# Reuse waits per tile instead of per pool in a four-layer network on one core

## The chip, the core and the metric

The kernel runs on one core of one Trainium2 chip. The metric is the device time of one execution in microseconds (us), the median of several runs. An execution under the hardware profiler gives the trace from which all views of the profile are taken. Engines are named as the profile names them: PE is TensorE (PEld its weight loads), DVE is VectorE, ACT is ScalarE, POOL is GpSimd, and SP issues most of the DMAs. DMAs can also be issued from ACT's and POOL's queues.

## What is computed

The input x has 8 blocks of 512 tokens with 128 features, all float32. Four layers follow, each "macaron" style: half of a feed-forward network is added, then attention, then the same feed-forward network once more by half. In outline:

```python
for layer in range(4):
    x = x + 0.5 * ffn[layer](layernorm(x))
    x = x + attn[layer](layernorm(x))
    x = x + 0.5 * ffn[layer](layernorm(x))
```

The parts differ by layer:

- Layer 0: attention with 16 heads of 8 and a learned bias by relative position (clipped at 128 either way), whole 512 x 512 softmax. Its feed-forward part has 8 experts of 176, top 2, and a shared expert of 352.
- Layer 1: causal attention with 16 heads, value width 64. Its feed-forward part holds a small attention over 8 columns, a layer normalisation and 8 experts of which one is applied to each token.
- Layer 2: an associative scan over the tokens (two 128 x 128 products and an RMS normalisation per combination) in place of softmax attention. Its feed-forward part sends each token to one of 8 experts of 512 with a squared ReLU.
- Layer 3: full attention with 16 heads. Its feed-forward part has 64 experts of 96, top 8 with a capacity of 64 tokens for each expert, and a shared expert. Tokens beyond an expert's capacity are dropped.

## The kernel before

The residual X stays in SBUF as one tile of 128 partitions x 32 token tiles x 128 features for the whole run. A block is four token tiles. All stages run on all 8 blocks, one stage after another, as run() (L2069) lists them. Start times in the trace: ffn0 (0, with attention0's preparations between its steps), attention0 (378), ffn0 (1179), ffn1 (1517), attention1 (1861), ffn1 (2520), ffn2 (2862), attn2 (3089), ffn2 (3257), ffn3 (3437), attention3 (3622), ffn3 (4230), end (4418).

**Pools.** Each stage opens pools of SBUF tiles and a pool of PSUM banks and closes them at its end. The next stage's pools are laid over the memory that the last one left. Within a pool a tag names a ring of buffers (`bufs`), handed out in program order. A few pools live throughout: `const` (X, identity, weight slot a), `small` (statistics of the normalisations `ln_mv`, `ln_st`, `ln_rs`, two buffers each, L145 and L158 to L169) and `dram` (tables in DRAM). `late` holds weight slot b from the second ffn0 on.

**What waits.** A framework, Tile, puts the semaphores. When a pool covers memory of closed pools, the pool's tiles wait by default until the whole of those pools is released, that is, until the last instruction that used any tile of them has ended. Data that passes through X, and tiles of a living pool, have waits of their own in either case.

**What orders the instructions.** The kernel's code gives a program order. Tile schedules from it with a list scheduler, which may put an instruction of one engine ahead of an earlier one where nothing that it waits for stands against it, with the earlier lines going first. In the trace, L824 of attention3 (a copy of a bias out of slot b) runs at 2852.33, in ffn1. Each engine works its own list in order.

The lines that the prediction's steps touch:

- `stats` and `scale` (L158 to L175): a block's mean, variance, and the normalised tile `xn` of the next stage. `transpose4` (L180 to L188) turns it through a PSUM bank `mid` into `XT`.
- `ffn0` (L263): xn, gate, experts L323 to L335. PSUM pool `psum` from `banks` (L130): mid 2 banks, big 2 x 2, acc 2.
- `attention0` (L356, pools at L589): scores L501 in `ps_s`, transposes L525 and products L542 in banks of their own.
- `ffn1` (L1008): `half`, `spread_v`, then xn at L1040 (on ACT), transposes L1047, products L1073. Blocks are taken in two halves of four columns.
- `attention1` (L600): `mask` at L619 is the first tile, then statistics and xn; its output projections are L771.
- `ffn2` (L1349): statistics in a pool of its own (`s2`), a sort of the tokens by expert through DRAM (L1504), expert weights `wt` fetched on SP's queue (L1500), sorted tokens (L1525), copies `xst` (L1546), up L1553, ReLU L1559, down L1573, results added to X (L1612).
- `attn2` (L1627): pools `a2` (the sequences `seq0` and on) and `a2b` (xn and temporaries).
- `ffn3` (L1709): pools `f3` (`zero`, `keys` and other single tiles) and `f3b` (normalised tokens `xw`, weights of the experts, gathered tokens). `zero` is filled on POOL (L1723), and `clear` (L1742) writes it from ACT's queue over the DRAM table `parts`, two transfers of 1 MB for each of the first three blocks. The routing (L1771 to L1777) follows, then the experts, and at the end `collect` in the pool `f3c` (L2006 to L2021), which adds eight rows to each token. A second part of the routing and of the collection stands under a condition (`tc.If`) that is not taken here.
- `attention3` (L804): its own xn, a V tile filled by memset, and PSUM pool `ps3` with seven banks `one` and one `acc`.

Where tiles lie over each other, in kilobytes of a partition (worked out from the tile sizes, in the order of the pools): `ahead` 82.1 to 159.4, with PB's three buffers at 88.4 to 127.4. ffn0's XT 108.7 to 124.7 and f0's xn from 124.7. ffn1's `half`, xn and xt 108.7 to 122.7, hm 209.7 to 215.7. attention1's mask 108.7 to 110.7. ffn2's xn 124.7 to 140.8, s2 212.8 on (first time). attn2's seq0 124.7 to 140.8, a2b 156.7 to 170.8. ffn3's zero 124.7 to 132.7, f3b 154.7 to 220.7, f3c 124.7 to 152.7. attention3's V 124.7 to 140.7.

Of the kernel before, what the change touches and what calls it, by code (L numbers as in the profile page):

```python
# [65 lines left out]
class Slot:  # L66


    def __init__(self, flat):
        self.flat = flat  # L70
        self.off = 0
# [10 lines left out]
class Net:  # L82
    def __init__(self, ctx, tc, ins, out):
        self.tc, self.nc, self.ins, self.out = tc, tc.nc, ins, out
        nc = self.nc
        self.const = ctx.enter_context(tc.tile_pool(name="const", bufs=1))
        self.small = ctx.enter_context(tc.tile_pool(name="small", bufs=2))
        self.dram = ctx.enter_context(
            tc.tile_pool(name="dram", bufs=4, space=bass.MemoryType.DRAM)
        )  # L90
# [38 lines left out]
    @contextmanager  # L129
    def banks(self):  # L130

        with self.tc.tile_pool(name="psum", bufs=2, space=bass.MemoryType.PSUM) as p:
            self.psum = p
            yield
        self.psum = None

    @contextmanager
    def turned(self):

        with self.tc.tile_pool(name="turned", bufs=1) as p:  # L140
            self.XT = p.tile([P, NB, BT], F32, name="XT")
            yield
        self.XT = None
# [119 lines left out]
    def ffn0(self, ahead=()):  # L263

        nc, w = self.nc, self.w
        with self.tc.tile_pool(name="f0", bufs=2) as pool:
            wts = {}

            def prep(b):
# [86 lines left out]
    def attention0(self, pool, zero):  # L356
# [5 lines left out]
        with ExitStack() as ctx:  # L362
            psum = late = None
# [222 lines left out]
                at(4 * m + 6, lambda m=m: gather(m))  # L586
                at(4 * m + 8, lambda m=m: output(m))
            yield [f for n in range(-29, 0) for f in extra.get(n, [])]
            late = ctx.enter_context(self.tc.tile_pool(name="at0", bufs=2))  # L589
            psum = ctx.enter_context(self.tc.tile_pool(name="ps0", bufs=2, space=bass.MemoryType.PSUM))  # L590
            for n in range(N + 9):
                if n < N:
                    scores(n)
# [6 lines left out]
    def attention1(self):  # L600
# [2 lines left out]

        nc, w = self.nc, self.w
        with ExitStack() as ctx:
            pool = ctx.enter_context(self.tc.tile_pool(name="at1", bufs=2))
            psum = ctx.enter_context(self.tc.tile_pool(name="ps1", bufs=2, space=bass.MemoryType.PSUM))
            LAG, LAGV = 12, 3
            NU = NB * 4
            N = 8 * NU  # L610
# [193 lines left out]
    def attention3(self):  # L804
# [3 lines left out]

        nc, w = self.nc, self.w
        with ExitStack() as ctx:  # L810
            pool = ctx.enter_context(self.tc.tile_pool(name="at3", bufs=2))
            psum = ctx.enter_context(self.tc.tile_pool(name="ps3", bufs=1, space=bass.MemoryType.PSUM))
            self.psum = psum
            LAG, LAGV = 12, 3
            NU = NB * 4
# [192 lines left out]
    def ffn1(self):  # L1008
        nc, w = self.nc, self.w
        scale = 1.0 / math.sqrt(HD)  # L1010
        with ExitStack() as ctx:
            pool = ctx.enter_context(self.tc.tile_pool(name="f1", bufs=2))
            psum = ctx.enter_context(self.tc.tile_pool(name="ps1", bufs=2, space=bass.MemoryType.PSUM))

            def mid():
                return psum.tile([P, BT], F32, name="ps_mid", tag="mid", bufs=3)
# [332 lines left out]
    def ffn2(self, with_polar):  # L1349
# [3 lines left out]
        nc, w = self.nc, self.w  # L1353
        NE, KT, HC = 8, 39, 4
        with ExitStack() as ctx:
            pool = ctx.enter_context(self.tc.tile_pool(name="f2", bufs=2))
            small, self.small = self.small, ctx.enter_context(self.tc.tile_pool(name="s2", bufs=2))
            self.psum = ctx.enter_context(self.tc.tile_pool(name="ps2", bufs=2, space=bass.MemoryType.PSUM))
            extra = self.polar_steps(pool) if with_polar else []
            xs_table = self.table2  # L1360

# [264 lines left out]

    def attn2(self):  # L1627
        nc, w = self.nc, self.w
        with self.tc.tile_pool(name="a2", bufs=1) as pool, self.tc.tile_pool(name="a2b", bufs=2) as pool2:
            eps = pool.tile([P, 1], F32, name="eps")  # L1630
            nc.gpsimd.memset(eps, EPS_RMS)
            lens = [BT + 1]
# [76 lines left out]
    def ffn3(self, last):  # L1709
# [6 lines left out]
        ROWS = K3 * NTOK  # L1716
        HALF = NTOK // 2
        SOON = 3
        with self.tc.tile_pool(name="f3", bufs=1) as pool, self.tc.tile_pool(name="f3b", bufs=2) as pool2:
            table = self.table  # L1720
            parts = self.dram.tile([ROWS + NTOK, D], F32, name="parts", tag="parts", bufs=1)
            zero = pool.tile([P, 16 * D], F32, name="zero")
# [283 lines left out]
            fetch(1)  # L2006
            interleave([lambda n=n: group(n) for n in range(8)], [lambda i=i: shared(i) for i in range(NB + 3)])

        with self.tc.tile_pool(name="f3c", bufs=2) as pool:
            def collect(t):  # L2010
                c = pool.tile([P, K3, D], F32, name="co", tag="co", bufs=6)
                nc.sync.dma_start(
                    out=c.rearrange("p j d -> p (j d)"),
                    in_=parts[t * P * K3 : (t + 1) * P * K3, :].rearrange("(p j) d -> p (j d)", j=K3),
                )
                r = pool.tile([P, 4, D], F32, name="cr", tag="cr")
                nc.gpsimd.tensor_tensor(out=r, in0=c[:, 0:4, :], in1=c[:, 4:8, :], op=ALU.add)  # L2017
                nc.vector.tensor_tensor(r[:, 0:2, :], r[:, 0:2, :], r[:, 2:4, :], ALU.add)  # L2018
                nc.vector.tensor_tensor(r[:, 0, :], r[:, 0, :], r[:, 1, :], ALU.add)  # L2019
                x = self.X[:, t, :]  # L2020
                nc.vector.scalar_tensor_tensor(x, r[:, 0, :], 0.5, x, ALU.mult, ALU.add)  # L2021
                if last and t % 4 == 3:
                    self.store(t // 4)

            for t in range(4 * SOON):
                collect(t)
            with self.tc.If(more):
                for t in range(4 * SOON, NT):
                    collect(t)
# [38 lines left out]

    def run(self):  # L2069
        self.load("a", self.L0)  # L2070
        with self.tc.tile_pool(name="ahead", bufs=2) as ahead:
            with self.tc.tile_pool(name="blank", bufs=1) as pool:
                zero = self.ready2(pool)
                rest = self.attention0(ahead, zero.rearrange("p (k c) -> p k c", k=8))
                steps = next(rest)
                with self.turned(), self.banks():
                    self.ffn0(steps)
            for _ in rest:
                pass
        with self.tc.tile_pool(name="late", bufs=1) as late:  # L2080
            self.slots["b"] = late.tile([P, 6816], F32, name="slot_b")
            self.load("b", self.L1)
            with self.turned(), self.banks():
                self.ffn0()
            self.load("a", self.L2)
            self.ffn1()
            self.attention1()
            self.ffn1()
            self.load("b", self.L3)
            with self.turned():  # L2090
                self.ffn2(True)
                with self.banks():
# [148 lines left out]
```

## Time and profile before

| | |
|---|---|
| median of 3 runs | 4406.22 us (4403.34 to 4411.11) |
| profiled execution | 4419.59 us |
| its span in the trace | 4417.8 us |
| mean granted PE clock | 0.903 |
| ACT busy | 2086.6 us (47%) |
| POOL busy | 980.7 us (22%) |
| DMA | 331.79 MB, mean 75 GB/s |
| DMA `wt` (ffn2's expert weights) | 78 of 512 KB, 4.2 us to land |
| DMA `parts` from `zero` | 12 of 1024 KB, 11.7 us to land |

The page of the profile gives busy time for each engine, then the span in 40 slices of 110.4 us: a digit is the busy share in tenths (9 means 90% or more). PEclk in that table is the clock that TensorE was granted, in tenths of full speed. A line of the timeline has the start in us, the busy time, engine, line, operation, output and inputs, shape and count, and in brackets how long the engine had idled before it and what ended that. "DVEq" and "ACTq" are the queues of these engines, with register loads and DMA issues. A wait for several things is put down to the one that came last. In a row of the windows view, the stretch and its length are followed by busy time of PE, PEld, DVE, ACT and POOL with the count of instructions, the granted clock, DMA's busy share and GB/s.

### The profile page before, as it was taken

How to read it: one execution, taken by the hardware profiler on the slowest of the kernel's cores; microseconds unless marked ns; L12 is line 12 of the kernel's file. 1: busy time of each engine (PE TensorE's matmuls, PEld its weight loads, DVE VectorE, ACT ScalarE, POOL GpSimd, SP SyncE). 2: the span in 40 equal slices, each digit the busy share in tenths (PEclk: the TensorE clock that was granted, in tenths of full speed). 3: DMA queues.
4: the chain of work that ended last, by engine and by line, in shares of the span. 5: the costliest groups of instructions: out<-in, count | busy, mean ns of one | idle time of the engine just before them, and what ended most of it. 6: DMA issues, size and time to landing. Idle time of an engine off the chain costs nothing. (4 is left out here: it accounts for less than half of the span.)

```text
span 4417.8 us, 64316 instructions
## 1 busy us (share of the span) xinstructions
PE 3785.8 (86%) x23046; PEld 2065.0 (47%) x23046; DVE 2765.6 (63%) x7495; ACT 2086.6 (47%) x4422; POOL 980.7 (22%) x1270
## 2 busy tenths in 40 slices
PE   8999999999999868899999967868667359999946
PEld 3445666666544345434344444467347233333324
DVE  5655777777756566656656466656553556777654
ACT  2335877878533324377877623312213015555521
POOL 1001111111000265211111266143024350000026
PEclk9999999999999979989999979969668579999967
DMA  6006777777300000000000000035007430000035
GB/s 256 0 5 203 220 226 221 223 221 225 93 1 1 5 0 1 1 1 1 1 1 1 1 0 2 8 100 172 0 13 239 153 125 1 1 1 1 1 109 169
DMA packets 217613, 331.79 MB, mean 75 GB/s; under 512 B 19954, under 2 KB 188380, under 8 KB 213700
## 3 DMA queue, kind: packets, MB, share of 16 engines
q1 hardware_dynamic: 197284, 290.59, 20.5%
q0 software_dynamic: 9664, 19.84, 1.5%
q10 hardware_dynamic: 10336, 17.17, 1.0%
q8 instruction: 183, 3.00, 0.3%
q14 instruction: 146, 1.20, 0.1%
HBM read 182.71 MB, written 144.82 MB: 74 GB/s over the span
## 5 line engine op out<-in xcount | busy, mean ns | idle before, releaser
L509 DVE CUSTOM_DVE_ANT_0 ps_s<-ps_s,PB 128x512 f32<-128x512 f32 x512 | 352.3, 704 | 155.5 <-PE ps_s L501 73.8
L901 DVE TENSOR_REDUCE nm<-ps_one 128x1 f32<-128x512 f32 x512 | 328.9, 685 | 155.4 <-PE ps_one L895 140.3
L513 ACT ACTIVATE pn<-ps_s,nm 128x512 f32<-128x512 f32 x512 | 356.8, 697 | 104.8 <-DVE nm L509 104.8
L907 ACT ACTIVATE pt<-ps_one 128x512 f32<-128x512 f32 x512 | 277.6, 595 | 203.7 <-PE ps_one L895 157.8
L168 POOL TENSOR_TENSOR ln_rs<-ln_rs,mhalf 128x4 f32<-128x4 f32 x128 | 132.7, 1037 | 897.5 <-DVE ln_rs L167 887.4
L895 PE MATMUL ps_one<-KT,QT 32*128 32x512 f32 x1024 | 307.5, 662 | 0.8 <-ACT KT L857 0.8
L675 ACT ACTIVATE sc<-sc,nm 128x512 f32<-128x512 f32 (+3 forms) x512 | 285.8, 562 | 39.5 <-DVE nm L732 33.3
L525 PE MATMUL ps_one<-ident,pn 128*128 128x128 f32 x2048 | 293.3, 282 | 12.2 <-DVE y L562 9.8
L732 DVE CUSTOM_DVE_ANT_0 sc<-ps_one,mask 128x512 f32<-128x512 f32 (+3 forms) x512 | 232.3, 487 | 105.5 <-PE ps_one L723 86.3
L887 PE MATMUL ps_one<-Q,KT 32*128 32x512 f32 x1024 | 289.7, 639 | 0.0
L326 ACT ACTIVATE sg<-ps_big 128x512 f32<-128x512 f32 x224 | 132.3, 597 | 320.2 <-PE ps_big L324 300.0
L450 PE MATMUL ps_one<-rdiff,QT 32*128 32x256 f32 x940 | 267.4, 404 | 14.5 <-ACT pt L528 14.4
L525 PEld LDWEIGHTS ps_one<-ident,pn 128*128 128x128 f32 x2048 | 219.1, 141 | 122.2 <-ACT pn L513 37.4
L327 DVE TENSOR_TENSOR sg<-sg,ps_big 128x512 f32<-128x512 f32 x224 | 152.3, 684 | 194.1 <-ACT sg L326 192.4
L739 ACT ACTIVATE pt<-ps_one 128x512 f32<-128x512 f32 (+3 forms) x512 | 209.6, 431 | 101.0 <-PE ps_one L723 92.9
L323 PE MATMUL ps_big<-XT,slot_a 128*128 128x512 f32 x448 | 236.7, 610 | 12.2 <-DVE sg L327 12.2
L501 PE MATMUL ps_s<-KT,QT 32*128 32x512 f32 (+2 forms) x1024 | 237.3, 540 | 0.8 <-ACT E L454 0.7
L324 PE MATMUL ps_big<-XT,slot_a 128*128 128x512 f32 x448 | 233.2, 602 | 0.0
L723 PE MATMUL ps_one<-KT,QT 32*128 32x512 f32 (+3 forms) x1024 | 229.7, 494 | 3.5 <-ACT pt L739 2.8
L715 PE MATMUL ps_one<-Q,KT 32*128 32x512 f32 (+3 forms) x1024 | 226.2, 483 | 6.8 <-ACT KT L662 5.8
L335 PE MATMUL ps_acc<-h,slot_a 128*128 128x512 f32 x448 | 229.8, 596 | 0.4 <-DVE h L329 0.4
L456 POOL COPY E<-E 128x127 f32<-128x127 f32 (+1 forms) x256 | 88.6, 346 | 637.2 <-ACT E L454 631.5
(436 smaller groups left out, 8386.1 us busy)
## 6 DMA issues: line engine op xcount, KB each, us to landing
rel_rows<-E SPq DMA_DIRECT2D x192, 383.0 KB, 3.7
PB<-rel_rows SPq DMA_DIRECT2D x128, 384.0 KB, 3.4
wt<-in_f_w_dram SPq DMA_DIRECT2D x78, 512.0 KB, 4.2
PB<-rel_rows SPq DMA_DIRECT2D x128, 256.0 KB
table<-blank SPq DMA_DIRECT2D x16, 1032.0 KB, 17.8
rel_rows<-E SPq DMA_DIRECT2D x64, 256.0 KB, 3.2
parts<-zero ACTq DMA_DIRECT2D x12, 1024.0 KB, 11.7
co<-parts SPq DMA_DIRECT2D x24, 512.0 KB, 7.1
```

The source lines that it names most:

```text
L323: nc.tensor.matmul(out=gu[:, 0, :], lhsT=w["f0_g"][:, cs], rhs=self.XT[:, b, :], start=True, stop=True)
L324: nc.tensor.matmul(out=gu[:, 1, :], lhsT=w["f0_u"][:, cs], rhs=self.XT[:, b, :], start=True, stop=True)
L450: nc.tensor.matmul(out=ps[:, c * 256 : c * 256 + 256], lhsT=Q[u][rr, i * P : (i + 1) * P], rhs=rdiff[rr, :], start=True, stop=True, tile_p ...
L501: nc.tensor.matmul(out=s[:, k, far:BT], lhsT=qt[rr, i * P : (i + 1) * P], rhs=kt[rr, far:BT], start=True, stop=True, tile_position=(32 * g ...
L509: nc.vector.tensor_tensor_reduce(out=s[:, k, :], in0=s[:, k, :], in1=pb[:, k, PB_AT[i] : PB_AT[i] + BT], scale=-1.0, scalar=1e30, op0=ALU. ...
L513: nc.scalar.activation(pn[:, k, :], s[:, k, :], AF.Exp, bias=nm[:, k : k + 1], scale=-1.0)
L525: nc.tensor.transpose(ps[:, j * P : (j + 1) * P], pn[:, k, j * P : (j + 1) * P], self.ident)
L675: nc.scalar.activation(sc[:, k, 0:wd], sc[:, k, 0:wd], AF.Exp, bias=maxs[u % 2][:, i, g, HD : HD + 1], scale=-1.0, accum_out=SUMS[u][:, i, ...
L887: nc.tensor.matmul(out=tw[k], lhsT=K[uw][rr, j * P : (j + 1) * P], rhs=Q2[uw][rr, :], start=True, stop=True, tile_position=(32 * g, 0),)
L895: nc.tensor.matmul(out=ts[k], lhsT=Q[u][rr, i * P : (i + 1) * P], rhs=K[u][rr, :], start=True, stop=True, tile_position=(32 * g, 0),)
L901: nc.vector.tensor_reduce(maxs[u % 2][:, i, 2 * hp + k : 2 * hp + k + 1, HD], ts[k], AX.X, ALU.max, negate=True)
L907: nc.scalar.activation(PT[m][:, k, :], tw[k], AF.Exp)
```

## The change

Nearly every pool is opened with `reuse_waits="tile"`. With it, a tile that is laid over memory of a closed pool waits for the accesses to those old tiles whose bytes or banks it covers, and not for the whole pool. No computation, size, address or program order is edited. Of the pools, two keep the default: `a2b` (L1629) and `f3b` (L1719). The diff, cut to one place of each kind:

```diff
-        self.const = ctx.enter_context(tc.tile_pool(name="const", bufs=1))
-        self.small = ctx.enter_context(tc.tile_pool(name="small", bufs=2))
+        self.const = ctx.enter_context(tc.tile_pool(reuse_waits="tile", name="const", bufs=1))
+        self.small = ctx.enter_context(tc.tile_pool(reuse_waits="tile", name="small", bufs=2))
...
-        with self.tc.tile_pool(name="psum", bufs=2, space=bass.MemoryType.PSUM) as p:
+        with self.tc.tile_pool(reuse_waits="tile", name="psum", bufs=2, space=bass.MemoryType.PSUM) as p:
...
-            pool = ctx.enter_context(self.tc.tile_pool(name="f1", bufs=2))
-            psum = ctx.enter_context(self.tc.tile_pool(name="ps1", bufs=2, space=bass.MemoryType.PSUM))
+            pool = ctx.enter_context(self.tc.tile_pool(reuse_waits="tile", name="f1", bufs=2))
+            psum = ctx.enter_context(self.tc.tile_pool(reuse_waits="tile", name="ps1", bufs=2, space=bass.MemoryType.PSUM))
...
-        with self.tc.tile_pool(name="a2", bufs=1) as pool, self.tc.tile_pool(name="a2b", bufs=2) as pool2:
+        with self.tc.tile_pool(reuse_waits="tile", name="a2", bufs=1) as pool, self.tc.tile_pool(name="a2b", bufs=2) as pool2:
...
-        with self.tc.tile_pool(name="f3", bufs=1) as pool, self.tc.tile_pool(name="f3b", bufs=2) as pool2:
+        with self.tc.tile_pool(reuse_waits="tile", name="f3", bufs=1) as pool, self.tc.tile_pool(name="f3b", bufs=2) as pool2:
...
-        with self.tc.tile_pool(name="f3c", bufs=2) as pool:
+        with self.tc.tile_pool(reuse_waits="tile", name="f3c", bufs=2) as pool:
```

The same edit stands at `dram`, `turned`, `f0`, `at0`, `ps0`, `at1`, `ps1` (twice), `at3`, `ps3`, `f2`, `s2`, `ps2`, `ahead`, `blank` and `late`.

More of the change, by code (lines that the diff above doesn't have):

```diff
@@ L85, in __init__ @@
         nc = self.nc
-        self.const = ctx.enter_context(tc.tile_pool(name="const", bufs=1))
-        self.small = ctx.enter_context(tc.tile_pool(name="small", bufs=2))
+        self.const = ctx.enter_context(tc.tile_pool(reuse_waits="tile", name="const", bufs=1))
+        self.small = ctx.enter_context(tc.tile_pool(reuse_waits="tile", name="small", bufs=2))
         self.dram = ctx.enter_context(
-            tc.tile_pool(name="dram", bufs=4, space=bass.MemoryType.DRAM)
+            tc.tile_pool(reuse_waits="tile", name="dram", bufs=4, space=bass.MemoryType.DRAM)
         )
@@ L138, in turned @@
     def turned(self):
-        with self.tc.tile_pool(name="turned", bufs=1) as p:
+        with self.tc.tile_pool(reuse_waits="tile", name="turned", bufs=1) as p:
             self.XT = p.tile([P, NB, BT], F32, name="XT")
@@ L265, in ffn0 @@
         nc, w = self.nc, self.w
-        with self.tc.tile_pool(name="f0", bufs=2) as pool:
+        with self.tc.tile_pool(reuse_waits="tile", name="f0", bufs=2) as pool:
             wts = {}
@@ L588, in attention0 @@
             yield [f for n in range(-29, 0) for f in extra.get(n, [])]
-            late = ctx.enter_context(self.tc.tile_pool(name="at0", bufs=2))
-            psum = ctx.enter_context(self.tc.tile_pool(name="ps0", bufs=2, space=bass.MemoryType.PSUM))
+            late = ctx.enter_context(self.tc.tile_pool(reuse_waits="tile", name="at0", bufs=2))
+            psum = ctx.enter_context(self.tc.tile_pool(reuse_waits="tile", name="ps0", bufs=2, space=bass.MemoryType.PSUM))
             for n in range(N + 9):
@@ L605, in attention1 @@
         with ExitStack() as ctx:
-            pool = ctx.enter_context(self.tc.tile_pool(name="at1", bufs=2))
-            psum = ctx.enter_context(self.tc.tile_pool(name="ps1", bufs=2, space=bass.MemoryType.PSUM))
+            pool = ctx.enter_context(self.tc.tile_pool(reuse_waits="tile", name="at1", bufs=2))
+            psum = ctx.enter_context(self.tc.tile_pool(reuse_waits="tile", name="ps1", bufs=2, space=bass.MemoryType.PSUM))
             LAG, LAGV = 12, 3
@@ L810, in attention3 @@
         with ExitStack() as ctx:
-            pool = ctx.enter_context(self.tc.tile_pool(name="at3", bufs=2))
-            psum = ctx.enter_context(self.tc.tile_pool(name="ps3", bufs=1, space=bass.MemoryType.PSUM))
+            pool = ctx.enter_context(self.tc.tile_pool(reuse_waits="tile", name="at3", bufs=2))
+            psum = ctx.enter_context(self.tc.tile_pool(reuse_waits="tile", name="ps3", bufs=1, space=bass.MemoryType.PSUM))
             self.psum = psum
@@ L1011, in ffn1 @@
         with ExitStack() as ctx:
-            pool = ctx.enter_context(self.tc.tile_pool(name="f1", bufs=2))
-            psum = ctx.enter_context(self.tc.tile_pool(name="ps1", bufs=2, space=bass.MemoryType.PSUM))
+            pool = ctx.enter_context(self.tc.tile_pool(reuse_waits="tile", name="f1", bufs=2))
+            psum = ctx.enter_context(self.tc.tile_pool(reuse_waits="tile", name="ps1", bufs=2, space=bass.MemoryType.PSUM))
             def mid():
@@ L1355, in ffn2 @@
         with ExitStack() as ctx:
-            pool = ctx.enter_context(self.tc.tile_pool(name="f2", bufs=2))
-            small, self.small = self.small, ctx.enter_context(self.tc.tile_pool(name="s2", bufs=2))
-            self.psum = ctx.enter_context(self.tc.tile_pool(name="ps2", bufs=2, space=bass.MemoryType.PSUM))
+            pool = ctx.enter_context(self.tc.tile_pool(reuse_waits="tile", name="f2", bufs=2))
+            small, self.small = self.small, ctx.enter_context(self.tc.tile_pool(reuse_waits="tile", name="s2", bufs=2))
+            self.psum = ctx.enter_context(self.tc.tile_pool(reuse_waits="tile", name="ps2", bufs=2, space=bass.MemoryType.PSUM))
             extra = self.polar_steps(pool) if with_polar else []
@@ L2070, in run @@
         self.load("a", self.L0)
-        with self.tc.tile_pool(name="ahead", bufs=2) as ahead:
-            with self.tc.tile_pool(name="blank", bufs=1) as pool:
+        with self.tc.tile_pool(reuse_waits="tile", name="ahead", bufs=2) as ahead:
+            with self.tc.tile_pool(reuse_waits="tile", name="blank", bufs=1) as pool:
                 zero = self.ready2(pool)
@@ L2079, in run @@
                 pass
-        with self.tc.tile_pool(name="late", bufs=1) as late:
+        with self.tc.tile_pool(reuse_waits="tile", name="late", bufs=1) as late:
             self.slots["b"] = late.tile([P, 6816], F32, name="slot_b")
```

## The prediction

> **What bounds the kernel.** I read the engine totals first, then the 40 slices.
>
> ```profile
> span 4417.8 us, 64316 instructions
> ...
> PE 3785.8 (86%) x23046; PEld 2065.0 (47%) x23046; DVE 2765.6 (63%) x7495; ACT 2086.6 (47%) x4422; POOL 980.7 (22%) x1270
> ...
> PE   8999999999999868899999967868667359999946
> ...
> PEclk9999999999999979989999979969668579999967
> ```
>
> The reader should see two things. TensorE (PE) is busy 86% of the span, and where it reads 9 no pool wait can cost anything: the stage is bound by matmuls. The rest of the span, 632 us of idle PE, lies in the handovers from stage to stage, at slice 15, in slices 24 to 33 and in the last two; there the clock row falls too. The change can only act where a first tile of a new stage waits for the last user of old memory, so I then read the timeline at each handover of run().
>
> Releasers in these lines say what came last, not what was needed:
>
> ```profile
> 1178.55 0.86 DVE L175 TENSOR_SCALAR xn<-X,ln_mv,ln_rs 128x128 f32<-128x128 f32 x3 [2.01 <-PE ps_av L542]
> 1516.74 1.65 ACT L1040 ACTIVATE xn<-X,ln_nmr,ln_rs 128x128 f32<-128x128 f32 x4 [0.89 <-PE ps_mid L211]
> 1861.83 0.52 POOL L619 MEMSET mask<- 128x512 f32 x1 [1.77 <-DVE ln_mv L165]
> 2520.30 3.18 ACT L1040 ACTIVATE xn<-X,ln_nmr,ln_rs 128x128 f32<-128x128 f32 x8 [9.46 <-PE ps_one L771]
> 3622.38 3.57 DVE L175 TENSOR_SCALAR xn<-X,ln_mv,ln_rs 128x128 f32<-128x128 f32 x4 [0.61 <-DVEq L2027]
> 4230.72 1.80 POOL L1723 MEMSET zero<- 128x2048 f32 x1 [46.55 <-PE ps_one L955]
> ```
>
> In each, a memset or a normalisation that reads only X and its statistics starts as the old stage's last product or transpose ends. Neither reads that product; the memory is all they share. That is the wait to be split.
>
> **The change, handover by handover.** Nothing is computed that was not computed before; what may move is when first tiles are written. That work does move up when it may: in the trace L824 (attention3's `a_qb`) runs at 2852.33, in the middle of ffn1. What holds it afterwards is the last of three: the tile it covers, its PSUM bank, its data. The `small` tags (two buffers) are handed out in program order as well.
>
> 1. ffn0 to attention0 (378): the scores wait for the last E (L454), whose mid banks 0 and 1 are also the scores' first banks. 1.5 us; ends 0 and 2.
> 2. attention0 to ffn0 (1179): xn lies over PB buffers last read near 1167, and the mid banks are free by 1173.5. PE idles 0.46+0.69+0.72 = 1.9 us around its first transposes, and then runs four pairs L323/L324 at 1.73 to 2.06 us against 1.02, which is 3.6 more. 5.5 us; ends 0 and 7.
> 3. ffn0 to ffn1 (1517): f1's xn lies over XT, last read at 1511.9, so half 0 (its four tiles are final) can go. Tile 28 of X is final only at 1517.3. 4 us; ends 0 and 5.4 (1517.3 less 1511.9).
> 4. ffn1 to attention1 (1861): the mask covers `half`, read until 1861.2, and the statistics' small tags are taken until then. 1 us; ends 0 and 2.
> 5. attention1 to ffn1 (2520): ACT idled 9.46 us before xn. X of those tiles is long final, but the three mid banks were used by the last projections, free at 2515.2, 2518.1 and 2520.5, and PE works to 2520.2. xn, its copies and the next transposes move up by 4.5 us; ends 0 and 9.5.
> 6. ffn1 to ffn2 (2862): PE idles 8.21 us before 2868.66. DVE waits there for X of the last blocks, but the first four blocks are final by 2850, and the s2 statistics lie over hm buffers read until about 2858. DVE's start at 2865.05 moves under the tail. 4.5 us; ends 0 and 8.2.
> 7. ffn2 to attn2 (3089): `a2b` (L1629) is not given the option; its xn waits as before. 0.5 us; ends 0 and 1.
> 8. attn2 to ffn2 (3257): xn covers seq0, read until 3255.3. 1.5 us; ends 0 and 2.
> 9. ffn2 to ffn3 (3437): `f3b` keeps the old wait, so xw (L175 at 3437.87) stays. What moves is `zero`, in `f3`, and with it six clears of `parts` on ACT's queue.
>
> ```profile
> 3437.71 1.80 POOL L1723 MEMSET zero<- 128x2048 f32 x1 [0.73 <-DVE X L1612]
> 3441.93 10.72 ACTq L1742 DMA_DIRECT2D parts<-zero  x6
> 3453.15 0.42 DVE L1777 TENSOR_REDUCE r_s<-p 128x4 f32<-128x256 f32 x1 [7.43 <-ACT p L1771]
> ```
>
> These hold ACT for 10.72 us and through its exp leave DVE idle 7.43: that goes, 7.4 us gained. But `zero` covers ffn2's normalised tokens, last read by the sort at 3328, so the six may go at about 3332, beside the first experts. Two windows of ten microseconds show what they meet (PE, PEld, DVE, ACT, POOL busy, then clock, DMA share, GB/s):
>
> ```profile
> 3330.00:3340.00 10.00, 4.27 (x14) 2.77 (x14) 0.59 (x4) 1.18 (x2) 0.00 (x0) 0.50 0.63 178
> 3390.00:3400.00 10.00, 9.84 (x89) 9.65 (x88) 3.84 (x8) 4.66 (x8) 3.90 (x5) 1.00 0.98 326
> ```
>
> Six clears write 6.29 MB: 14.8 us of all DMA engines at the 426 GB/s of their own window, 19.3 at 326. From 3340 on the share is 0.92 to 1.00 and PE takes weights as they come (2.44 us waited for wt at 3337). Behind the clears in ACT's order stand the copies of sorted tokens (3334.79) and the relus (from 3339.28), for which PE waits. DMA is idle 3.7 of the 10 us to 3340, so I take 11 us lost (14.8 less 3.7). Net -3.5 us; ends +7.4 (they land after 3410, where the share is 0.32) and -18 (10.72 of ACT and 14.8 of DMA in turn, less 7.4).
>
> [...]
>
> 10. ffn3 to attention3 (3622): xn, transposes and the memsets of V may pass the last collect, but DVE is busy 8.3 of 10 us there and 9.0 in the next ten. Of ten microseconds I count 4; ends 0 and 10.
> 11. attention3 to ffn3 (4230): the clears lie over V of an early block and can go out while DMA is idle; the 3.51 us for which DVE waited at 4243.24 and part of the 1.80 memset go. xw keeps its wait. 4.5 us; ends 0 and 5.3.
>
> The sum is 1.5+5.5+4+1+4.5+4.5+0.5+1.5-3.5+4+4.5 = 28 us. The profiled execution took 4419.59 us (span 4417.8, 1.8 around it) and would take 4391.6: 0.63% less. On the median of 4406.22 this makes **4378**. All items at their good ends make 60 us; all at their bad ones, -18.
>
> **The clock at the handovers.** Two windows after the one at 1861 (same columns, five microseconds each):
>
> ```profile
> 1875.00:1880.00 5.00, 5.00 (x8) 1.00 (x6) 3.13 (x15) 4.00 (x16) 0.00 (x0) 0.50 0.00 0
> 1895.00:1900.00 5.00, 5.00 (x12) 1.66 (x15) 2.24 (x10) 1.97 (x8) 0.00 (x0) 0.50 0.00 0
> ```
>
> PE is busy throughout and the granted clock is still 0.50; it rises near 1903. So a shorter gap does not by itself bring the clock back, and I count none of it in the sum, except the four pairs of item 2. [...]
>
> **Rivals.**
> *A, little moves.* The small tags' order, the banks of the last products and the true data on X hold the first tiles about as long as the pool did. For it: items 1, 4, 7 and 8, where this is what I read. Against: 2, 3, 5, 11. Then some 5 us come back: 4401. That the option moves no instruction at all ends here too, at 4406.
> *B, slower.* The clears' landing place decides. If all six leave between 3332 and 3343 ahead of the copies in ACT's order, both prices are paid: -18 us. If at the same time the other ten give under 9, the time is over 4415; with 5 from A, 4419. It decides from the point where the clears reach ACT before 3334.79. For it: ACT idles 24.99 us before that point, and `zero` is free. Against: items 2, 5, 6, 11 would all have to fail.
> *C, the clock.* If the shorter gaps keep the clock up at 1865 to 1903, 2545 to 2575 and 3622 to 3655, some 100 us at half clock become about 60 (not all of it PE's): 40 us on top, 4338. Against: DVE is busy 7 to 9 tenths in the last two, and the gap at 1861 stays.
>
> **Chances.** The forecast (4351 to 4397) 0.58; A (4397 to 4415) 0.15; B (above 4415) 0.14; C (below 4351) 0.13. About 0.2%, 8.8 us, is what a measurement of this kernel tells from no change, so A is the middle class: faster 0.71, same 0.15, slower 0.14. The range leaves out half of B's and half of C's: 4338 to 4420; it takes in the good ends short of C and the bad end short of -14.
>
> **What would show it.** Right: xn at the second ffn0 before 1178; L1040 before 2520 less the shift up to there; the memset of `zero` under attention3; six clears at about 3332 in the first ffn3's case, DVE's wait of 7.43 gone, and wt's landing later. Wrong: L1040 still the first after the last product; clears still after X of L1612; or a new row among the waits in which PE waits for ACT L1546 near 3335 for 8 us or more. What would upset the whole is an order of instructions that changes inside the PE-bound stages, where 1% is 38 us and none of the rows above bears on it.

## The result and the profile after

The changed kernel takes 4398.1 us, the median of 20 runs (4383.77 to 4403.9); the kernel before took 4408.32 us beside it (20 runs, 4398.92 to 4418.63). The ratio is 0.9972, with a 95% interval of 0.9965 to 0.9979: 0.28%, which is 12 us by the ratio and 10 us by the two medians. The forecast, 28 us, had the side right and the size wrong. As the experiments show, most of what was gained came from something that was not in its sum.

The page of the changed kernel seems at first to say that 28 us was right, since its span is 28.9 us shorter than that of before:

```profile
span 4388.9 us, 64204 instructions
...
PE 3760.3 (86%) x23046; PEld 2058.3 (47%) x23046; DVE 2760.8 (63%) x7495; ACT 2085.9 (48%) x4422; POOL 981.3 (22%) x1270
...
PE   8999999999999958899999957968567369999946
...
PEclk9999999999999979999999979959668579999967
```

The reader should look at PE's busy time and its count. The same 23046 products take 25.5 us less (3785.8 to 3760.3); PE's idle time, which is what waits can give back, went from 632.0 to 628.6 us, 3.4 less. Nearly all of the difference between these two executions is the clock at which the same products ran (mean granted clock 0.903 before, 0.910 after).

The two traces, read side by side, explain the small idle part: **on every engine the two kernels have the same instructions in the same order.** (On PE a dozen of the 23046 records, all of products on 32 rows, change places.) Only semaphore waits differ. So the instructions that the forecast saw moved up did start earlier, each only up to the one ahead of it in its own engine's list. The timeline of the changed kernel, at the places that were shown of before:

```profile
1178.32 0.85 DVE L175 TENSOR_SCALAR xn<-X,ln_mv,ln_rs 128x128 f32<-128x128 f32 x3
1515.63 1.65 ACT L1040 ACTIVATE xn<-X,ln_nmr,ln_rs 128x128 f32<-128x128 f32 x4
1860.37 0.52 POOL L619 MEMSET mask<- 128x512 f32 x1 [1.23 <-DVE y L1263]
2498.72 1.64 ACT L1040 ACTIVATE xn<-X,ln_nmr,ln_rs 128x128 f32<-128x128 f32 x4
2509.31 1.04 PE L1047 MATMUL ps_mid<-ident,xn 128*128 128x128 f32 x8
3423.37 1.80 POOL L1723 MEMSET zero<- 128x2048 f32 x1
3607.57 2.27 DVE L175 TENSOR_SCALAR xn<-X,ln_mv,ln_rs 128x128 f32<-128x128 f32 x4 [0.56 <-DVEq L2027]
4156.40 1.80 POOL L1723 MEMSET zero<- 128x2048 f32 x1
4200.67 10.24 ACTq L1742 DMA_DIRECT2D parts<-zero  x4
4210.95 0.58 ACT L187 COPY XT<-ps_mid 128x512 f32<-128x512 f32 x1 [9.76 <-DMA f_u<-in_f_u_dram]
```

Beside them stand two lines of the kernel before:

```profile
2521.09 0.46 PE L1026 MATMUL ps_mid<-slot_b,spread_v 128*128 128x128 f32 x2 [0.88 <-DVE spread_v L1024]
2521.39 2.48 PE L1047 MATMUL ps_mid<-ident,xn 128*128 128x128 f32 x8
```

L1040 of the second ffn1 starts 21.6 us earlier than before (2520.30 to 2498.72). Everything at this place is 12 us earlier by then (PE's last run of projections, L771, from 2513.25 to 2501.24), so that 9.6 us of it are the thinner wait. But the transposes that read it (L1047) stand behind 60 projections in PE's list and begin only at 2509.31, which is 12.1 us earlier, as everything is; PE had idled 0.88 us in front of them and now idles 0.79. The second memset of `zero` runs 74 us earlier, 46.6 us of that beyond the 27.7 by which its neighbours moved. It now lies under attention3 and helps nobody: its clears stand behind attention3's last copy in ACT's list and are issued at 4200.67, where they hold the next copy for 9.76 us.

Since the order is the same, each product of one trace can be paired with the same product of the other, and the time between two of them compared. Means of three traces of each kernel (the first ones and p1 to p4 below), changed less before; another choice of the two products moves a row by about 1 us:

| handover (item of the prediction) | taken for the sum | measured | PE idle in it |
|---|---|---|---|
| 1 to attention0 | -1.5 us | +0.3 | +0.2 |
| 2 to the second ffn0 | -5.5 | -1.5 | -0.5 |
| 3 to ffn1 | -4 | 0.0 | +0.2 |
| 4 to attention1, 1840 to 1940 | -1 | **-9.2** | -0.6 |
| 5 to the second ffn1 | -4.5 | +0.5 | +1.4 |
| 6 to ffn2 | -4.5 | -0.2 | -0.6 |
| 7 to attn2 | -0.5 | -0.4 | -0.9 |
| 8 to the second ffn2 | -1.5 | -0.3 | -0.2 |
| 9 to ffn3 | +3.5 | -0.9 | -1.0 |
| 10 to attention3 | -4 | -1.0 | -1.1 |
| 11 to the second ffn3 | -4.5 | -0.1 | +0.5 |

The fourth handover gives 9.2 of the 12.8 us in this table, with half a microsecond less idle time. The rest of the 9.2 is clock. Five microseconds of the kernel before in attention1 and of the changed one (busy time of PE, PEld, DVE, ACT, POOL, then the granted clock, DMA share, GB/s):

```profile
1885.00:1890.00 5.00, 5.00 (x12) 1.34 (x12) 3.03 (x13) 2.45 (x10) 0.00 (x0) 0.50 0.00 0
```

```profile
1885.00:1890.00 5.00, 4.97 (x25) 1.99 (x24) 4.30 (x18) 4.05 (x13) 0.12 (x1) 1.00 0.00 0
```

PE is full in both; it works on twelve products at clock 0.50 and on twenty-five at 1.00. Before, this stretch at half clock lasts 27 us (1874 to 1901), with PE busy in all of it (27.31 of 27.31 us); after, it is not there. (Short pieces at half clock are in both: 3.4 us at 1908 before, 3.4 at 1894 and 6.8 at 1914 after.) In each of these two traces all records of the granted clock (74 before, 78 after) begin at whole multiples of 3.413 us from the first one, to within 0.01 us; the stretch is eight such steps long, the short pieces one, one and two. Below, a trace's grid is these times, and a boundary is one of them.

From this came the theory: half a microsecond less at one handover moves attention1's first products against that grid, and so takes away a stretch at half clock. The rivals: the gain is the sum of many small waits; or the stretches come and go by chance and only seem to belong to the change.

### The profile page after: what moved, and what is told of

It is laid out like the page before. It is cut to its first block, busy times and chain, and to the rows that moved or that the text cites. A ratio compares the mean times of both kernels' runs of the same rounds, so it can differ in the third digit from the quotient of the medians.

```text
span 4388.9 us, 64204 instructions
## 1 busy us (share of the span) xinstructions
PE 3760.3 (86%) x23046; PEld 2058.3 (47%) x23046; DVE 2760.8 (63%) x7495; ACT 2085.9 (48%) x4422; POOL 981.3 (22%) x1270
## 5 line engine op out<-in xcount | busy, mean ns | idle before, releaser
L168 POOL TENSOR_TENSOR ln_rs<-ln_rs,mhalf 128x4 f32<-128x4 f32 x128 | 133.0, 1040 | 896.1 <-DVE ln_rs L167 886.0
L895 PE MATMUL ps_one<-KT,QT 32*128 32x512 f32 x1024 | 300.7, 639 | 0.8 <-ACT KT L857 0.8
L723 PE MATMUL ps_one<-KT,QT 32*128 32x512 f32 (+3 forms) x1024 | 226.2, 484 | 3.6 <-ACT pt L739 2.8
```

What stands on the lines that cost most here:

```text
L895: nc.tensor.matmul(out=ts[k], lhsT=Q[u][rr, i * P : (i + 1) * P], rhs=K[u][rr, :], start=True, stop=True, tile_position=(32 * g, 0),)
```

## Experiments

By their traces, e1, e2, e3 and d1 have the order of instructions of before. In d2, d3, d4 and f1 the added instructions also put a few of DVE's statistics and normalisations right behind them into another order (27, 11, 25 and 9 places in DVE's list), and in e4 some hundred of DVE's places in ffn3's routing differ. A ratio is to the kernel before, run on the same chip.

**e1 and e2, halves of the change.** The option on PSUM pools alone, and on all the other pools alone:

```diff
 # e1: of the 23 pools that the change edits, only those with space=PSUM keep
+reuse_waits="tile"
 # e2: only those without
+reuse_waits="tile"
```

> The order of the instructions is the same as before on every engine; only waits differ. The per-tile option is kept on the PSUM pools alone. Theory (the changed waits save only what an engine idles directly in front of a thinned wait, and xn waits for SBUF tiles): ratio to before 0.999 to 1.000, no first xn starts earlier, and the xn of the second ffn1 stays behind the last projection. Rival (the banks of the last products are what held the first tiles): ratio 0.997 to 0.998. Second rival (all of the difference of the two traces is the stretches at half clock, which fall as they will): both ends of the clock, 4395 to 4420, in either half of the change.

> The other half: the option on the SBUF and DRAM pools, not on PSUM. Theory: nearly the whole effect, ratio 0.997 to 0.998; xn of the second ffn1 (L1040) starts some 20 us before the last projection ends, and PE is nonetheless only about 1 us earlier, since L1047 stands behind L771 in its order. Rival (banks): 0.999 to 1.000. If the halves add up to 0.997, nothing interacts.

e1: 4405.11 us, 0.9991 (0.9983 to 1.0). e2: 4404.12 us, 0.9989 (0.9979 to 0.9999). By its time e1 came as its theory had it, and e2 did not (0.997 to 0.998). Times alone tell little: the halves look alike, and their sum, 0.998, lies near the whole. The traces tell more. e1 has the 27 us stretch and e2 has not; from 1840 to 1940 e1 differs from before by +0.2 us, e2 by -10.8. So in these traces the SBUF waits do remove the stretch. Why e2's median doesn't show all of it stays open: its eleven runs spread from 4389 to 4411 us, its trace, one execution of 4404 us, has another long stretch, after the collect (below), and whether the first stretch comes back in others of its executions was not seen.

**e3 and e4, the two pools left out, and the clears on another queue.**

```diff
 # e3
-self.tc.tile_pool(name="a2b", bufs=2)
+self.tc.tile_pool(reuse_waits="tile", name="a2b", bufs=2)
-self.tc.tile_pool(name="f3b", bufs=2)
+self.tc.tile_pool(reuse_waits="tile", name="f3b", bufs=2)
 # e4: e3, and in clear()
-nc.scalar.dma_start(out=parts[r, :]...
+nc.sync.dma_start(out=parts[r, :]...
```

> The option on a2b and f3b as well, whose xn and xw kept the old wait; order again the same. Theory (fixed order): at 3089, 3437 and 4230 the first xn and xw stand in DVE's list behind the last results of the stage before, so at most 2 us more than the change as made, ratio 0.9965 to 0.9975. Rival (the two pools left out hold back the handovers, as item 7 has it with 5 us, and as much at each of the two ffn3): 10 to 14 us more, ratio 0.994 to 0.995.

> As the one before it, with the clears of parts issued from SP's queue in place of ACT's, so that nothing of ACT stands before or behind them. Theory (the clears' wait was real, and ACT's order hid what the option frees): the six clears of the second ffn3 start while attention3 still works, ACT's exp no longer waits behind them, and 5 to 10 us go beside the run before, ratio 0.994 to 0.996; the second stage's gain is the larger. Rival (DMA is the bound of the first expert's weights and of the rows written, whoever issues): within 2 us of the run before, or slower.

e3: 4396.42 us, 0.9978 (0.9967 to 0.9988). e4: 4395.06 us, 0.9975 (0.9965 to 0.9986). Neither can be told from the change, and e4 is within 2 us of e3, as its rival said, not 5 to 10 faster. In the traces the handovers to ffn3 do get shorter: 4.1 us at 3437 and 4.2 at 4230 in e3 (idle time of PE 4.1 and 3.4 less), 7.0 and 2.0 in e4. That is more than the theory's 2 us in all and less than the rival's 10 to 14. Both traces have the longer of two stretches at the collect, which costs more than this gain; that this is why it doesn't reach the medians is not shown. (p4 below, the changed kernel with the longer stretch, took 4401.4 us; these two took 4395.68 and 4394.79.) e4's clears on SP's queue stand behind the weights of the experts there, another list to wait in: the second six are issued at 4204.64.

**p1 to p4, the same two kernels profiled again.** No edit.

> The kernel before once more, one look, for its half-clock stretches. Theory (the stretch at 1884, 27 us at clock 0.50 with PE full, belongs to the handover to attention1 as it was, since PE's first transposes come 1.2 to 1.5 us after a boundary of the clock's 3.4 us grid; the one after 3622 changes from run to run): the stretch at 1884 is there again; the one at the last collect is 41 or 72 us long, and the time is 4407 with the one, 4419 with the other. Rival (both are chance): the first is missing in about half of the looks.

> The changed kernel once more, one look. Theory: no stretch at 1884, whatever the time; the one at the last collect is 41 us (time near 4389) or 72 (near 4400), the latter in about two of three. Rival (both are chance): the stretch at 1884 appears in about half of the looks.

> As p1_before: the third look at the kernel before. Theory: the stretch at 1884 again. Rival: as there.

> As p2_after: the third look at the changed kernel. Theory: none at 1884. Rival: as there.

Their times: 4407.96 and 4411.59 us (before), 4393.21 and 4401.4 us (changed). The 27 us stretch is in all three traces of the kernel before and in none of three of the changed one. The other, which begins when PE falls idle before the collect, ends either 5 to 7 us after attention3's first transposes or 35 us after them: 44 and 44 us long here against 72 in the first trace of before, and 44 and 72 against 41 in the first trace of the changed one. The first two traces at the same place, before and after:

```profile
3640.00:3645.00 5.00, 5.00 (x11) 1.51 (x10) 1.49 (x3) 0.69 (x1) 0.00 (x0) 0.50 0.00 0
```

```profile
3640.00:3645.00 5.00, 5.00 (x55) 1.70 (x47) 3.73 (x6) 2.69 (x6) 0.00 (x0) 1.00 0.00 0
```

It does come and go in both kernels, for about 12 us of time (from 3560 to 3700 the changed kernel's first trace takes 13.3 us less than that of before, about 1 us of it the handover's own, row 10 above). So the first stretch belongs to the change and the second doesn't. The two first traces had drawn opposite ends of the second: without that, their spans would differ by some 17 us and not by 28.9.

**d1, one wait alone.** The option on attention1's SBUF pool and nowhere else; in the whole program a single wait changes, that of the mask's memset.

```diff
-            pool = ctx.enter_context(self.tc.tile_pool(name="at1", bufs=2))
+            pool = ctx.enter_context(self.tc.tile_pool(reuse_waits="tile", name="at1", bufs=2))
```

> The kernel before with the option on one pool alone, attention1's SBUF pool. In the whole program one wait differs: that of POOL's memset of the mask (L619). Theory (half a microsecond less at this one handover puts PE's start on the other side of a boundary of the clock's grid): the stretch at 1884 is gone, PE's start after the last transposes is 0.5 to 0.6 us earlier and the time falls by 8 to 11 us, ratio 0.9975 to 0.9982. Rival (the change works by many small waits): 0.6 us, ratio 0.9997 to 1.0002, the stretch stays.

4395.46 us, 0.9971 (0.996 to 0.9982): as much as the change with all its pools, and a little more than the theory's 0.9975 to 0.9982. Its timeline and its window, with PE's line of the kernel before behind them:

```profile
1860.95 0.53 POOL L619 MEMSET mask<- 128x512 f32 x1 [1.23 <-DVE y L1263]
1864.31 1.15 PE L634 MATMUL ps_one<-ident,xn 128*128 128x128 f32 x4 [7.60 <-DVE xn L175]
```

```profile
1885.00:1890.00 5.00, 4.97 (x25) 1.95 (x24) 4.30 (x16) 4.00 (x14) 0.00 (x0) 1.00 0.00 0
```

```profile
1865.15 1.15 PE L634 MATMUL ps_one<-ident,xn 128*128 128x128 f32 x4 [8.10 <-DVE xn L175]
```

PE idles 7.60 us before L634, where before it idled 8.10, and the stretch is gone. The rival, many small waits, asked for 0.9997 or above and for the stretch to stay.

**d2, a later start with all the old waits.** Seven needless memsets of the same zeros on POOL, six of them ahead of POOL's first step of attention1's statistics (L168):

```diff
-            nc.gpsimd.memset(mask, 0.0)
+            [nc.gpsimd.memset(mask, 0.0) for _ in range(4)]
 ...
-                nc.gpsimd.memset(m, 0.0)
+                [nc.gpsimd.memset(m, 0.0) for _ in range(3)]
```

> The kernel before, all waits as they were, with six needless memsets of 0.48 us more on POOL in front of attention1's first statistics (they fill the same tiles with the same zeros). PE starts attention1 some 2.9 us later, so that it comes 0.6 us after a grid boundary, as in the changed kernel, and not 1.15. Theory: the stretch of 27 us is gone all the same; 9 saved less 2.9 spent, 5 to 7 us faster than before, ratio 0.998 to 0.999. Rival (an earlier start is what counts): 3 us slower, 1.0007.

4393.27 us, 0.9969 (0.9957 to 0.998). A kernel that only does more work, in almost the same order, and whose PE idles 10.80 us at this place and not 8.10, is as much faster as the change is, and more than the theory's 0.998 to 0.999. But its trace, an execution of 4406 us, had the stretch:

```profile
1885.00:1890.00 5.00, 5.00 (x12) 1.31 (x12) 2.95 (x13) 2.42 (x10) 0.00 (x0) 0.50 0.00 0
```

Two more executions were profiled (f2 and f3). They have one order of instructions with d2, so that nothing but the execution differs:

> The kernel before with six needless memsets, once more, one look. Its first look showed the 27 us stretch, in an execution of 4406 us, while nine of its twelve times lie below 4398. Theory (it starts near a boundary and falls on either side): no stretch at 1884 in an execution below 4398, the stretch in one above 4404. Rival (the six memsets save in some other way): the stretch is there in a fast one too.

> As the one before it, a third look. Theory and rival as there.

4393.93 and 4393.0 us, both without the stretch. From 1840 to 1940 they take 8.8 and 8.9 us less than before, though PE idles 2.9 us more in it. Two lines of f2:

```profile
1869.03 0.90 PE L634 MATMUL ps_one<-ident,xn 128*128 128x128 f32 x3 [10.80 <-DVE xn L175]
```

```profile
1885.00:1890.00 5.00, 5.00 (x24) 2.21 (x24) 4.39 (x18) 4.65 (x17) 0.00 (x0) 1.00 0.02 5
```

**d3, the changed kernel put back on the grid.** 

```diff
-                nc.gpsimd.memset(m, 0.0)
+                [nc.gpsimd.memset(m, 0.0) for _ in range(2)]
```

> The changed kernel with two needless memsets more on POOL at the same place, one in front of the first statistics, one behind them: PE's first transposes come 0.5 us later, 1.05 to 1.15 us after a grid boundary, as before. Theory: the stretch of 27 us is back, 9 to 10 us slower than the change, ratio to before 0.9995 to 1.0. Rival: 0.5 us slower than the change, ratio 0.997 to 0.998.

4406.57 us, 0.9995 (0.9985 to 1.0006): half a microsecond of needless work in front of attention1, with the few of DVE's places that it moves, loses the whole gain. The stretch is back:

```profile
1863.15 1.12 PE L634 MATMUL ps_one<-ident,xn 128*128 128x128 f32 x4 [8.11 <-DVE xn L175]
```

```profile
1885.00:1890.00 5.00, 5.00 (x14) 1.20 (x10) 3.08 (x11) 2.61 (x9) 0.00 (x0) 0.50 0.02 5
```

**d4 and f1, PE kept busy in the gaps.** The option on all pools, and products that nothing reads:

```diff
 # d4 only, in attention1, after the last transposes of ffn1
+            with self.tc.issue_after(getattr(self.turned_last, "ins", self.turned_last)): fill = mid(); [nc.tensor.matmul(out=fill, lhsT=self.ident, rhs=self.cst[:, 0:BT], start=True, stop=True) for _ in range(8)]
 ...
 # d4 and f1, in attention3
+            fill = mid(); [nc.tensor.matmul(out=fill, lhsT=self.ident, rhs=self.cst[:, 0:BT], start=True, stop=True) for _ in range(44)]
```

> The option on all pools, and matrix products that nothing reads to keep PE busy: 8 of 128x512 between ffn1's last transposes and attention1's first (idle 8.1 us before), 44 between the experts of the first ffn3 and attention3 (idle 40.2 us before). Theory (the half clock after these handovers comes of PE's idle time, and only its phase was changed by the waits): no half clock from 1861 to 1903 and none from 3588 to 3660, and with the stretch at the collect either way 5 to 15 us less than with the option on all pools, ratio 0.993 to 0.996. Rival (the clock falls for other reasons than PE's idle time): no less than with the option on all pools, ratio 0.9975 or above.

> The option on all pools, and the 44 products that nothing reads only between the first ffn3 and attention3; attention1's handover as in the change. Theory (the half clock after the collect comes of 40 us of idle PE, that after 1872 of what PE does just after the handover): no half clock around 3588 to 3660 in any case and none from 1874 to 1901, some 12 us less than the option on all pools has in its slower executions and about as much as in its faster ones; median 4380 to 4388, ratio 0.9945 to 0.9965, and a narrower spread. Rival (the products disturb as much as they save): 0.9975 or above.

d4: 4401.76 us, 0.9985 (0.9975 to 0.9995), as its rival had it (0.9975 or above). With products in the gap and the clock full through it (two products of L652 right behind it, at 1863.49, take 1.13 us, where two at 1871.28, at half clock, take 2.08), attention1 came to a stretch of 31 us at half clock all the same, from 0.6 us behind the start of its first score products on: in d4's window from 1885 the clock is 0.50 with PE 5.00 of 5. So the 8 us gap is not needed for that stretch, and the theory's wording in this expectation was wrong. It does not follow that idle time has no part in it, since d4 kept shorter gaps. The last of them stands in front of the score products, where PE idles longer than in any other kernel here (0.78 us):

```profile
1867.29 4.06 PE L723 MATMUL ps_one<-KT,QT 32*128 32x512 f32 x16 [1.82 <-DVE ln_mv L165]
```

After the collect d4 had no long stretch (3.4 us at 3616).

f1: 4393.5 us, 0.9961 (0.9948 to 0.9974), the lowest ratio of all, though its interval overlaps that of the change and its median is above the 4380 to 4388 that the theory asked for; its runs fall in two groups, four of 4380 to 4384 us and eight of 4388 to 4400. In f1's trace the clock is full while the fillers run and then falls for 27 us at attention3's start:

```profile
3590.00:3595.00 5.00, 5.00 (x13) 2.23 (x12) 4.69 (x12) 0.00 (x0) 2.53 (x2) 1.00 0.19 78
...
3615.00:3620.00 5.00, 5.00 (x12) 1.51 (x8) 4.49 (x9) 0.00 (x0) 0.00 (x0) 0.50 0.02 3
```

f1's rival of 0.9975 or above is out, and so is its theory that filling the gap removes the stretch after the collect in any case.

**What goes with the stretch, over all traces.** For each trace I took the time from the last grid boundary of the clock records to the first score product on 32 rows (L723 in attention1, L895 in attention3), and whether half clock went on for some 27 us or more behind it. (The expectations reckon from the first transposes instead; the score products were chosen with the traces at hand.) In attention1 the boundary lies at 1870.80 in the first trace of before and at 1869.87 in that of the changed kernel, and their products at:

```profile
1871.60 2.42 PE L723 MATMUL ps_one<-KT,QT 32*128 32x512 f32 x16 [0.78 <-ACT KT L662]
1870.11 2.42 PE L723 MATMUL ps_one<-KT,QT 32*128 32x512 f32 x16 [0.78 <-ACT KT L662]
```

| first product, us after a boundary | long stretch at half clock behind it |
|---|---|
| attention1, 0.20 to 0.44: changed kernel (3 traces), e2, e3, e4, d1, f1, f2, f3 | none in 10 traces |
| attention1, 0.74 to 1.02: before (3 traces), e1, d2, d3 | in all 6 |
| attention1, 2.78: d4 | yes |
| attention3, 0.21 to 1.32: 10 traces, both kernels among them | none |
| attention3, 1.91 to 3.25: 7 traces, both kernels among them | in all 7 |

In attention1 the offset is nearly the same in every trace of one kernel (0.74 to 0.80 before, 0.21 to 0.24 after), although the program starts at different places of the grid (the first boundary comes 0.30 to 2.48 us after the start of the three traces of before); only d2 differs between its traces (0.80 against 0.41 and 0.44 in f3 and f2). In attention3 the offsets lie anywhere from 0.21 to 3.25. In attention1, where the offset holds so still after 1860 us, 0.3 to 0.6 us of it went with 8.8 to 10.8 us of time in the traces that were compared (9.2 in the means of the change, 10.8 in e2, 8.8 and 8.9 in f2 and f3).

The offset alone is not the rule: 0.74 to 1.02 goes with the stretch in attention1, and 0.57 to 1.32 goes without it in attention3. Nor is it idle time alone. PE idles 0.78 us in front of these products in every kernel but d4, so that in attention1 a later offset also puts more of this idle time behind the boundary (PE is busy 2.54 of the 3.41 us behind 1870.80 before, and 3.08 behind 1869.87 after). But PE is busy 2.63 of 3.41 us both in e1's attention1 (behind 1866.14, with the stretch) and in p1's attention3 (behind 3630.44, without). What brings on the long stretch was not separated.

## Why the prediction failed

**The step that failed first is "That work does move up when it may".** The forecast concluded from L824, which runs a long way ahead of its stage, that first tiles would be scheduled up to the moment when tile, bank and data are free. The order of instructions did not change at all. To the three things that the forecast names (the tile it covers, its PSUM bank, its data) comes a fourth, the instruction's place in its engine's list, and the option changes only the time at which the one at the head of the list may go. So two of the signs of being right came (L1040 before 2520, the memset of `zero` under attention3) and brought next to nothing.

- Items 2, 3, 5, 6, 10 and 11 were each priced at the time by which memory came free earlier: 27 us together. They measured 2.3 us together, because what stands ahead in the same list ended no earlier. Item 5 is the clearest: 9.6 us earlier on ACT than its surroundings, nothing on PE. Item 2 was also added up wrong: its rows have three pairs above 1.02 us (2.06, 1.91 and 1.73), which is 2.6 us more and not 3.6.
- Item 9 and rival B rested on the clears leaving at 3332. They were issued at 3427, behind the routing's first copy. `zero` is written right at the end of the sum into X, as before (3423.37, which is 14.3 us earlier, as is everything around it). Neither the gain of 7.4 us nor the loss of 11 occurred: DVE still waits for the exp there, 8.20 us where it was 7.43. That the clears would cost the experts' weights of ffn2 those 11 us was the forecast's estimate and no run shows it, since they were never issued beside them; the handover came out 0.9 us shorter (row 9).
- Item 11 was right in that the memset went under attention3, and wrong in that the clears would follow it.
- Items 7, 9 and 11 said that `a2b` and `f3b` keep something back; e3 confirms it for `f3b` with 4 us at each of the two handovers to ffn3, and not for `a2b` (its handover is 0.4 us shorter in the change and in e3 alike).
- **Rival A**, little moves, is the size of what the waits did: some 4 us over the eleven handovers without the clock's part, near its 5. What held the rest was the order of the lists, which is not one of the three causes that it names.
- **Rival C**, the clock, brought the gain, at the very place that it named (1865 to 1903), for another reason. It asked for a shorter gap that keeps the clock up. The half clock right at the handover (10 us) is there in both kernels. What went is the second stretch, and it went with the phase at which the products came: a longer gap does as well (f2 and f3), and a gap filled with products did not help (d4). No run shows its 40 us: the one stretch of 27 us that went was worth 9.2.
- The prediction read the rows of 0.50 with PE 5.00 of 5 correctly as something that a shorter gap need not end, and then left it out of the sum. The right conclusion would have been a term of either sign: a stretch of 27 us at half clock, 9.2 us of time here, that a shift of half a microsecond may take away or bring.
- The first two spans, 28.9 us apart, agree with the forecast of 28 by accident: 9 us of this are the stretch of rival C, some 12 the chance stretch at the collect, only 3.4 idle time, and the rest clock in small pieces elsewhere (such as 2 us each at the second ffn0 and in attn2).

What stays open: why products on 32 rows that start 0.7 us after a boundary are followed by 27 us at half clock, and those at 0.3 are not, while in attention3 those at 1.3 are not either; what keeps the offset so still in attention1; why the ratios of d1 and d2 make 13 us where the stretch makes 9; and why e2, whose trace is without the stretch, has a median above the change's.

## What to carry to other kernels

Compare the order of instructions before pricing a wait: the order stayed here, and the change gave back no more than 1.1 us of PE's idle time at any handover, since what stood ahead in the same list ended no earlier. Before believing a difference below 1% in a kernel bound by TensorE, split it into PE's busy time for the same products (clock) and PE's idle time (waits), in several executions of each. And try a change at the place with the sign turned: here a needless delay did as well as the removed wait, which no theory of waits gives.

## What was not expected of the hardware

- In the first trace of the kernel before, TensorE was busy for 27.31 of 27.31 us from 1874.22 on, at clock 0.50 all the while. In the first trace of each kernel the records of the clock begin at whole multiples of 3.413 us from one another (74 and 78 records). In attention1 0.5 us of phase went with 9.2 us of time; in attention3 phases of 0.2 to 1.3 and of 1.9 to 3.3 us went with times some 12 us apart.
- The times of one kernel fall in two parts: runs of the kernel before at 4399 to 4410 us and at 4412 to 4418, with mean clocks of 0.905 to 0.909 and 0.903 to 0.906 (32 runs beside d1 to d4). That the parts belong to such stretches is likely from the clocks, but not shown, since these runs have no traces.
- With products that nothing reads in the wait before attention3 (f1, d4) the clock was 1.00 from 3590 to 3595 and from 3600 to 3605, where it was 0.50 in the first traces of both kernels, and in f1 it still fell to 0.50 for 27 us in the stage that follows (in d4 for 3.4).
